# Pairwise outer products with batch norm: how the samples of long rows are cut into stores

## The chip, the cores and the metric

The kernel runs on one core of a Trainium2 chip. The metric is the device time of one execution in microseconds (us); of several executions the median is given.

## The reference, cut to what matters

```python
B, F0, F1, E, C = (256, 39, 39, 16, 1)          # the inputs here have a batch of 1024
_ROWS, _COLS = np.tril_indices(F1, k=-1)        # 741 pairs (row, col) with col < row
cross = xj[:, rows, :, None] * xi[:, cols, None, :]
mean = jnp.mean(cross, axis=(0, 2, 3), keepdims=True)
var = jnp.mean(jnp.square(cross - mean), axis=(0, 2, 3), keepdims=True)
normed = (cross - mean) * jax.lax.rsqrt(var + BN_EPS)
normed = normed * gamma[None, :, None, None] + beta[None, :, None, None]
out = normed[:, :, None, :, :] * W[None, None, :, :, :]
return jnp.transpose(out, (0, 2, 1, 3, 4))
```

xi and xj are 1024 x 39 x 16 in float32. For each of the 741 pairs of fields the outer product of two vectors of 16 is made, normalised with the pair's mean and variance over the batch, and multiplied with a 16 x 16 weight. The output is 1024 x 1 x 741 x 16 x 16, 777 MB, against 6 MB of input. In the output of one sample the pairs of a row r (r pairs: columns 0 to r-1) lie side by side, 1 KB a pair.

## The kernel before, in words

Each of the 128 partitions holds 8 samples. The moments of all pairs are worked out first (until about 40 us), from sums and small matmuls; each pair then has a scale s and a shift t in `st_sb`. What remains is, for each pair and sample, (xi * s) outer xj, plus t, times W, and the store.

**Tiles.** A tile is one row r for two samples of each partition (T = 2): `tiles[n] = (r, t0, place)`. `y_sb` has two slots of 76 pair-places (1 KB a partition each). Tiles 0 to 3 are row 19, tiles 4 to 11 rows 20 and 18; `FIRST_PIECES` sets the cuts of the first eight. From tile 12 on the order is row 38 (four tiles, one for each pair of samples), then rows 37 and 1, 36 and 2, 35 and 3, and so on to 21 and 17, the long row and its short partner together filling a slot. Slots alternate, so a tile's place was used last by the tile before the previous one.

**Steps of a tile.** The program is written in its final order; each engine runs its instructions in that order.

- `scale_xi(n + 2)`: GpSimd multiplies xi with s into an `xs` tile (line 169).
- `finish(n)`: adds t, multiplies by W and stores. For rows over `LONG` (33) ScalarE adds t to 8 pairs in the middle of the row (line 275) and GpSimd multiplies them by W in two steps of four pairs (line 280). For rows 33 and less GpSimd does both for the last 4 pairs or so (lines 277 and 280). All other pairs are VectorE's, one instruction a pair for both samples (line 291), in the order of the pairs.
- `products(n + 1)`: for sample 0, then sample 1, one instruction for each of 16 values of xj; ScalarE does the first 11 or 12 (line 147), GpSimd the rest (line 149). Rows of 4 and less are done by VectorE alone (lines 182 and 192).

**Stores.** SP issues all stores (line 216), in the order of `finish`, on one DMA queue. `bounds(n)` says where a row is cut: two pieces for rows 31 to 38, one for shorter rows. `store(n, c0, c1)` is called at the end of each piece, for the pairs c0 to c1. For a row above 19 from tile 8 on, sample 0 is stored piece by piece and sample 1 in one store behind the last piece:

```python
            if whole and step == 1 and t == t_to - 1:
                if c1 < r:
                    continue
                c0 = 0
```

So a tile of rows 31 to 38 has three stores: first piece of sample 0, second piece of sample 0, all of sample 1. A row below 19 has one store for both samples. In memory one store is one run of bytes for each partition and sample, and the trace has one packet for each such run.

**What sets the order around the change.** Products into a slot wait until the stores of the slot's previous pairs have landed, for each sample's pairs by themselves. A piece's store waits until VectorE and, where its pairs are among them, GpSimd are through with the piece. Products of a sample wait for nothing else of the other sample.

Of the kernel before, what the change touches and what calls it, by code (L numbers as in the profile page):

```python
# [15 lines left out]

ONE, LONG = 30, 33
FIRST_PIECES = (  # L20
    (0, 1, 3, 6, 10, 14, 19), (0, 4, 9, 14, 19), (0, 4, 11, 19), (0, 9, 19), (0, 10, 20), (0, 9, 18), (0, 10, 20), (0, 9, 18)
)
# [18 lines left out]
def tile_pair_outer_batchnorm(  # L41
# [95 lines left out]
    def view(n):  # L137
        r, _, u = tiles[n]
        return y_sb[:, u : u + T * r, :].rearrange("p (t n) e -> p t n e", t=T)
# [65 lines left out]
    def store(n, c0, c1, t_from=0, t_to=T):  # L205
        r, t0, _ = tiles[n]
        n0 = first[r]

        whole = n >= len(FIRST_PIECES)
        step = 1 if r > mid and (whole or c1 == r) else t_to - t_from  # L210
        for t in range(t_from, t_to, step):
            if whole and step == 1 and t == t_to - 1:
# [3 lines that stand above are left out]
            nc.sync.dma_start(  # L216
                out_v[:, t0 + t : t0 + t + step, (n0 + c0) * EE : (n0 + c1) * EE],
                view(n)[:, t : t + step, c0:c1, :].rearrange("p t n e -> p t (n e)"),
            )
# [14 lines left out]
    def weigh(n):  # L234

        y = view(n)
        for c0, c1 in zip(bounds(n), bounds(n)[1:]):
            affine(n, range(c0, min(c1, OWN)), (nc.vector,))
            nc.vector.tensor_tensor(  # L239
                y[:, :, c0:c1, :],  # L240
                y[:, :, c0:c1, :],
                w_dve.unsqueeze(1).to_broadcast([P, T, c1 - c0, EE]),
                ALU.mult,
            )
            store(n, c0, c1)

    def bounds(n):
        if n < len(FIRST_PIECES):
            return FIRST_PIECES[n]
        r = tiles[n][0]  # L250
        pieces = 1 + (r > ONE)
        return tuple(q * r // pieces for q in range(pieces + 1))

    def finish(n):

# [32 lines left out]
        for t in range(0, T, size):  # L288
            for c0, c1 in zip(bounds(n), bounds(n)[1:]):
                for c in [*range(c0, min(c1, p0)), *range(max(c0, p1), c1)]:  # L290
                    stt(  # L291
                        y[:, t : t + size, c, :],
                        y[:, t : t + size, c, :],
                        t_sb[:, n0 + c : n0 + c + 1],
                        w_dve.to_broadcast([P, size, EE]),
                        ALU.add,
                        ALU.mult,
                    )
                store(n, c0, c1, t, t + size)
# [262 lines left out]
```

## Time and profile before

| | |
|---|---|
| median of 4 runs | 1879.26 us (1879.16 to 1880.51) |
| the profiled execution's own time | 1879.28 us |
| its span, first to last instruction or transfer | 1877.6 us |
| VectorE busy | 1723.9 us, 92% |
| ScalarE busy | 1645.8 us, 88% |
| GpSimd busy | 1535.7 us, 82% |
| SP's DMA queue | 779.72 MB in 52320 packets, busy 97.9% of 16 engines' span |
| mean DMA rate over the span | 417 GB/s |

The page is of one execution, taken by the profiler. "Busy" is the time in which an engine executes instructions; DMA shares are those of the core's 16 DMA engines together. A row of the windows view gives a stretch of the span, the busy time of each engine with the number of instructions, the granted TensorE clock, and the share and rate of the DMA engines, where a packet counts in the stretch in which it starts; so a short stretch can show a share a little above 1, or one that is low because long packets began before it. A row of the waits view gives who waited for whom, the total in us, how often, and the longest. The page's table of DMA issues gives the time from a store's issue to its landing, which includes the time it stands in the queue behind others.

### The profile page before, as it was taken

How to read it: one execution, taken by the hardware profiler on the slowest of the kernel's cores; microseconds unless marked ns; L12 is line 12 of the kernel's file. 1: busy time of each engine (PE TensorE's matmuls, PEld its weight loads, DVE VectorE, ACT ScalarE, POOL GpSimd, SP SyncE). 2: the span in 40 equal slices, each digit the busy share in tenths (PEclk: the TensorE clock that was granted, in tenths of full speed). 3: DMA queues.
4: the chain of work that ended last, by engine and by line, in shares of the span. 5: the costliest groups of instructions: out<-in, count | busy, mean ns of one | idle time of the engine just before them, and what ended most of it. 6: DMA issues, size and time to landing. Idle time of an engine off the chain costs nothing.

```text
span 1877.6 us, 9638 instructions
## 1 busy us (share of the span) xinstructions
PE 26.0 (1%) x130; PEld 23.3 (1%) x130; DVE 1723.9 (92%) x2640; ACT 1645.8 (88%) x3416; POOL 1535.7 (82%) x1746
## 2 busy tenths in 40 slices
PE   5000000000000000000000000000000000000000
PEld 4000000000000000000000000000000000000000
DVE  8999888899999999999999999999999999999994
ACT  8999888888888899989999999998999998989892
POOL 8999778787877788888888888888888888888882
DMA  5999999999999999999999999999999999999998
GB/s 200 386 420 424 406 423 425 424 429 426 425 428 426 425 428 426 427 426 425 422 425 432 425 426 431 424 431 424 432 424 431 423 431 428 427 428 426 427 430 349
DMA packets 53690, 783.63 MB, mean 417 GB/s; under 512 B 4720, under 2 KB 6384, under 8 KB 17008
## 3 DMA queue, kind: packets, MB, share of 16 engines
q1 hardware_dynamic: 52320, 779.72, 97.9%
q10 hardware_dynamic: 1296, 3.29, 0.5%
q14 instruction: 73, 0.60, 0.1%
q8 instruction: 1, 0.02, 0.0%
HBM read 6.00 MB, written 776.99 MB: 417 GB/s over the span
## 4 chain that ended last, share of the span: by engine, by line
DMA 55%; ACT 20%; DVE 18%; issue 3%; POOL 2%; SPq 0%; ACTq 0%; DVEq 0%; PE 0%; POOLq 0%
DMA out_dram<-y_sb 55%; ACT y_sb L147 20%; DVE y_sb L291 17%; POOL y_sb L149 1%; DVE y_sb L358 1%; POOL xs L169 0%; ACT y_sb L230 0%; DVE y_sb L332 0%; SPq L216 0%; DMA xi_sb<-in_r_xi_dram 0%; POOL y_sb L277 0%; POOL y_sb L280 0%; POOL y_sb L342 0%; DVE y_sb L192 0%; DVE xs L182 0%
## 5 line engine op out<-in xcount | busy, mean ns | idle before, releaser
L291 DVE SCALAR_TENSOR_TENSOR y_sb<-y_sb,st_sb,w_dve 128x512 f32<-128x512 f32 (+1 forms) x2511 | 1653.2, 739 | 117.4 <-issue 103.8
L147 ACT ACTIVATE y_sb<-xs,xj_sb 128x288 f32<-128x288 f32 (+20 forms) x3194 | 1514.8, 567 | 181.5 <-DMA out_dram<-y_sb 148.4
L149 POOL TENSOR_SCALAR y_sb<-xs,xj_sb 128x480 f32<-128x480 f32 (+27 forms) x1126 | 607.2, 564 | 14.1 <-DMA out_dram<-y_sb 14.0
L280 POOL TENSOR_TENSOR y_sb<-y_sb,w_sb 128x2048 f32<-128x2048 f32 (+3 forms) x155 | 517.8, 3347 | 87.2 <-ACT y_sb L275 77.6
L169 POOL TENSOR_TENSOR xs<-xi_sb,st_sb 128x640 f32<-128x640 f32 (+33 forms) x135 | 184.2, 1364 | 197.1 <-ACT y_sb L147 193.3
L277 POOL TENSOR_SCALAR y_sb<-y_sb,st_sb 128x512 f32<-128x512 f32 x291 | 197.6, 695 | 5.1 <-ACT y_sb L147 5.1
L275 ACT ACTIVATE y_sb<-y_sb,st_sb 128x512 f32<-128x512 f32 x160 | 100.2, 708 | 4.0 <-POOL y_sb L149 2.3
L192 DVE TENSOR_TENSOR y_sb<-xs,ps 128x256 f32<-128x256 f32 (+3 forms) x32 | 24.8, 817 | 0.5
L489 PE MATMUL ps<-y_sb 39*128 39x38 f32 (+37 forms) x76 | 16.4, 397 | 2.8 <-DVE y_sb L475 2.8
L489 PEld LDWEIGHTS ps<-y_sb 39*128 39x128 f32 x76 | 16.3, 329 | 3.1 <-DVE y_sb L475 3.1
L353 ACT ACTIVATE y_sb<-y_sb 128x1248 f32<-128x1248 f32 x8 | 9.9, 1243 | 2.8 <-POOL y_sb L342 1.5
L358 DVE TENSOR_REDUCE y_sb<-y_sb 128x78 f32<-128x1248 f32 x8 | 11.2, 1445 | 0.4 <-ACT y_sb L353 0.4
L147 ACT ACTIVATE y_sb<-xi_sb,xj_sb 128x304 f32<-128x304 f32 x24 | 11.4, 537 | 0.0
L342 POOL TENSOR_TENSOR y_sb<-xi_sb,y_sb 128x1248 f32<-128x1248 f32 x4 | 9.2, 2324 | 2.2 <-ACT y_sb L391 2.2
L239 DVE TENSOR_TENSOR y_sb<-y_sb,w_dve 128x2048 f32<-128x2048 f32 (+4 forms) x6 | 10.7, 1839 | 0.1
L332 DVE TENSOR_REDUCE y_sb<-xi_sb 128x39 f32<-128x624 f32 (+1 forms) x6 | 6.1, 1012 | 3.7 <-DMA xi_sb<-in_r_xi_dram 3.7
L342 POOL TENSOR_TENSOR y_sb<-xj_sb,y_sb 128x1248 f32<-128x1248 f32 x4 | 9.2, 2320 | 0.0
L378 PE MATMUL ps<-y_sb 128*39 128x79 f32 x48 | 8.1, 340 | 15.3 <-DVE y_sb L358 15.1
L232 POOL TENSOR_SCALAR y_sb<-y_sb,st_sb 128x512 f32<-128x512 f32 x8 | 6.5, 817 | 2.1 <-ACT y_sb L147 2.1
L332 DVE TENSOR_REDUCE y_sb<-xj_sb 128x39 f32<-128x624 f32 (+1 forms) x6 | 6.1, 1015 | 0.6 <-DMA xj_sb<-in_r_xj_dram 0.6
L230 ACT ACTIVATE y_sb<-y_sb,st_sb 128x512 f32<-128x512 f32 x9 | 6.5, 802 | 0.2 <-ACT y_sb L147 0.2
L378 PEld LDWEIGHTS ps<-y_sb 128*39 128x39 f32 x48 | 5.8, 178 | 17.3 <-DVE y_sb L358 10.5
(59 smaller groups left out, 37.4 us busy)
## 6 DMA issues: line engine op xcount, KB each, us to landing
out_dram<-y_sb SPq DMA_DIRECT2D x25, 2304.0 KB, 10.4
out_dram<-y_sb SPq DMA_DIRECT2D x12, 3840.0 KB, 21.7
out_dram<-y_sb SPq DMA_DIRECT2D x21, 2048.0 KB, 12.5
out_dram<-y_sb SPq DMA_DIRECT2D x12, 3584.0 KB, 23.1
out_dram<-y_sb SPq DMA_DIRECT2D x12, 3328.0 KB, 24.4
out_dram<-y_sb SPq DMA_DIRECT2D x12, 3072.0 KB, 25.2
out_dram<-y_sb SPq DMA_DIRECT2D x16, 2176.0 KB, 11.0
out_dram<-y_sb SPq DMA_DIRECT2D x8, 4352.0 KB, 24.1
```

The costliest lines, as they stand in the source:

```text
L147: nc.scalar.activation(y, src, AF.Copy, scale=scale)
L149: engine.tensor_scalar(y, src, scale, 1.0, ALU.mult, ALU.mult)
L169: nc.gpsimd.tensor_tensor(xs, xi_sb[:, t0 : t0 + T, 0:r, :], s_sb[:, :, n0 : n0 + r, :].to_broadcast([P, T, r, E]), ALU.mult,)
L192: nc.vector.tensor_tensor(view(n)[:, t].rearrange("p n (i j) -> p n i j", j=E), xs[:, t].unsqueeze(2).to_broadcast([P, r, E, E]), xj_short ...
L275: nc.scalar.activation(y[:, :, c, :], y[:, :, c, :], AF.Identity, bias=t_c)
L277: nc.gpsimd.tensor_scalar(y[:, :, c, :], y[:, :, c, :], t_c, 1.0, ALU.add, ALU.mult)
L280: nc.gpsimd.tensor_tensor(y[:, :, c0:c1, :], y[:, :, c0:c1, :], w_sb.unsqueeze(1).to_broadcast([P, T, c1 - c0, EE]), ALU.mult,)
L291: stt(y[:, t : t + size, c, :], y[:, t : t + size, c, :], t_sb[:, n0 + c : n0 + c + 1], w_dve.to_broadcast([P, size, EE]), ALU.add, ALU.mult,)
L342: nc.gpsimd.tensor_tensor(devs[n % 7], sources[x][:, t0 : t0 + T], shift[:, x : x + 1, :].unsqueeze(3).to_broadcast([P, T, F, E]), ALU.sub ...
L358: nc.vector.tensor_reduce(to[:, t0 : t0 + T, F : 2 * F], devs[n % 7], AX.X, ALU.add)
L378: nc.tensor.matmul(ps_g[acc][0:F, 0 : 2 * F + 1], lhs, fb[:, t], start=t == 0, stop=t == NT - 1)
L489: nc.tensor.matmul(ps[:, :, first[r] - n0 : first[r] - n0 + r], pick[:, r, :], stq[:, :, 0:r], start=True, stop=True,)
```

## The change

Two things in how rows are cut, and nothing in what is computed.

- `store`: the constant `WHOLE` = 36 keeps the scheme "sample 1 in one store" for rows up to 36. In rows 38 and 37 the first piece is now one store for both samples (128 partitions x 2 runs), and the second piece is one store for each sample. These tiles still have three stores.
- `bounds`: in rows 36 to 31 the first piece has 19, 20, 21, 22, 23 and 24 pairs in place of 18, 17, 17, 16, 16 and 15. Rows 38 and 37 are cut as before, at 19 and 18.

```diff
-ONE, LONG = 30, 33
+ONE, LONG, WHOLE = 30, 33, 36
...
-        whole = n >= len(FIRST_PIECES)
+        whole = n >= len(FIRST_PIECES) and r <= WHOLE
         step = 1 if r > mid and (whole or c1 == r) else t_to - t_from
...
         r = tiles[n][0]
-        pieces = 1 + (r > ONE)
-        return tuple(q * r // pieces for q in range(pieces + 1))
+        if r <= ONE:
+            return 0, r
+
+        return 0, r // 2 + max(0, (WHOLE + 1 - r) * 3 // 2), r
```

The order of all instructions on every engine stays as it was, the stores' included; the new file has two more lines inside `bounds`, so the lines behind it are two higher (275 is 277, 280 is 282, 291 is 293), while 147, 149, 169 and 216 stay.

## The prediction

> **What bounds the kernel now.** I read the page first: the span and the DMA rows.
>
> ```profile
> span 1877.6 us, 9638 instructions
> ...
> DMA packets 53690, 783.63 MB, mean 417 GB/s; under 512 B 4720, under 2 KB 6384, under 8 KB 17008
> ## 3 DMA queue, kind: packets, MB, share of 16 engines
> q1 hardware_dynamic: 52320, 779.72, 97.9%
> ```
>
> One queue, SP's, is busy for 97.9% of sixteen engines' span. VectorE with 92% and ScalarE with 88% are high too, but the question is who waits for whom. So the waits come next, ScalarE's first:
>
> ```profile
> ACT y_sb L147 <- DMA out_dram<-y_sb: 148.4, 79, 4.5
> ```
>
> ScalarE's products wait for stores to free their half of y_sb. The loop is closed by the store stream: stores free the buffer, the buffer lets products start, products lead to stores. An edit counts only where it changes the stream's bytes, packets or gaps. For the gaps I cut the steady part into windows (columns: stretch, length, busy time of PE, PEld, DVE, ACT, POOL, clock, DMA share, GB/s):
>
> ```profile
> 191.50:193.30 1.80, 0.00 (x0) 0.00 (x0) 1.03 (x2) 1.80 (x4) 0.35 (x1) 1.00 0.00 0
> 193.30:240.00 46.70, 0.00 (x0) 0.00 (x0) 39.68 (x60) 39.06 (x59) 37.53 (x26) 1.00 1.00 427
> 240.00:240.40 0.40, 0.00 (x0) 0.00 (x0) 0.00 (x0) 0.40 (x1) 0.00 (x0) 1.00 0.00 0
> 240.40:380.00 139.60, 0.00 (x0) 0.00 (x0) 124.01 (x195) 118.94 (x180) 109.58 (x78) 1.00 1.01 427
> 640.00:930.00 290.00, 0.00 (x0) 0.00 (x0) 272.69 (x413) 264.02 (x605) 244.82 (x314) 1.00 1.01 426
> 1500.00:1866.00 366.00, 0.00 (x0) 0.00 (x0) 327.66 (x495) 305.64 (x696) 286.08 (x365) 1.00 1.00 428
> ```
>
> The stream runs at 426 to 428 GB/s everywhere but in two holes, both among the tiles of row 38, where the share is 0.00. Rows 36 to 31 (370 to 930 us) show no hole. The last view is the end, where the share falls although every store is issued:
>
> ```profile
> 1868.00:1870.00 2.00, 0.00 (x0) 0.00 (x0) 0.00 (x0) 0.00 (x0) 0.00 (x0) 1.00 0.27 113
> 1872.00:1874.00 2.00, 0.00 (x0) 0.00 (x0) 0.00 (x0) 0.00 (x0) 0.00 (x0) 1.00 0.10 44
> ```
>
> The trace's sixteen completion marks of each store explain it: twelve engines are done with the last store at 1868.2 to 1868.6, the others up to 1876.7. So the engine that is last sets the end. That engine is late by 0.2 us at 340, by 2 to 3 at 700 to 930 and by 8.4 at the end. A gap hurts only if it reaches that engine.
>
> **Part 1: rows 38 and 37, gain.** The first tile of row 38 starts its finish at 172.69. Its first piece is issued at 184.38 (2432 KB, landing 7.3 us later, at 191.7), its second at 192.56. Landing trails the last packet by 0.4 (the last packet of all ends at 1876.2, its mark is at 1876.7), so the queue is dry from 191.3 until the second piece's first packet at 193.4 (issue 0.33, then 0.5): 2.1 us for all engines. With the change the store at 184.38 carries both samples' first halves, 4864 KB. A half of 2432 KB is 19-KB packets, 8 an engine; at 732 ns each that is 5.9 us, so two last 11.7, from 185.2 to 196.9. The other two issues are where they were (192.56 and 192.94). The hole is gone: -2.1, with -1.8 (the empty window alone) as the lower bound. The hole at 240 is the same thing in the third tile: the piece issued at 231.46 takes 9.2 us, so its last packet ends at 240.2, and the next one starts at 239.64 + 0.33 + 0.5 = 240.5. That is 0.2 for the last engine (0.4 by the window). Together -2.3, between -1.8 and -2.5.
>
> **Part 2: packets, cost.** Row 38 and 37 tiles had three packets a partition (two short, one of the whole sample), and get four short ones: 128 more for each of 8 tiles, 1024, or 64 an engine. The trace's packet records give 1448.4 ns for 38912 B and 731.6 for 19456 B (means), so a cut costs 2 x 731.6 - 1448.4 = 14.8 ns. 64 x 14.8 = +0.95 us. From the fastest packets it is 2 x 721 - 1436 = 6 ns, +0.4; I take the means, since most packets run in a full stream. The number of DMA instructions stays three a tile, and SP's queue holds them in the same order.
>
> The Trainium skill has a rule against such cuts: its page "DMA: Bandwidth & Descriptors" (section Bandwidth, Measured) puts a floor of about 10.5 ns on a packet. By it the 64 packets would be 0.67 us, an estimate from that page, and the forecast 0.3 us lower. The page's figure is for small loads, the row is for these stores, so the row stands.
>
> **Part 3: sample 0 comes free later, cover.** ScalarE and GpSimd make products of sample 0 first. Before, sample 0 of a tile left the queue in its first half of bytes; now it leaves after three quarters, 5.9 us later relative to the tile's end. Sample 1's time does not move. Before, ScalarE found sample 0 free and waited 2.5 to 4.4 us before sample 1 (rows at 211.96, 234.94 and 258.46); that wait moves ahead of sample 0 and becomes longer. On ScalarE's queue the sample-1 products stand behind it and then the next tile's eight L275 steps; VectorE and GpSimd wait for those. Worked out for row 38, from the landing of sample 0: 2 x 7.73 (eleven products each) + 0.1 + 11.7 (finish start to first store, 172.69 to 184.38; GpSimd's two L280 steps end last) + 0.83 (issue to first packet) = 28.1. The stream has from that landing the last piece (5.9) and the whole next tile (four such halves, 23.4), less the 0.4 by which landing trails: 28.9. Spare 0.8; with row 37's products of 7.57 it is 1.1. Before, the tightest place was the second piece, with nothing spare at 240. So the cover is thin but whole: 0, and if it is gone the loss is the overrun, once in two tiles.
>
> **Part 4: rows 36 to 31, later first pieces, cover.** First pieces grow from 18, 17, 17, 16, 16, 15 pairs to 19, 20, 21, 22, 23, 24. For rows 36 to 34 VectorE's share becomes 11, 12 or 13 pairs (x 0.66 = 7.3 to 8.6 us), still earlier than GpSimd's 11.7, so the issue does not move. For rows 33, 32 and 31 VectorE alone decides, and the issue moves by 6, 7 and 9 pairs: 4.0, 4.6 and 5.9 us. The cover is the queue ahead of them. A store into an idle queue lands 7.2 us after issue where its packets take 5.9, so 1.3 is overhead. The first pieces of row 33 land 11.7 to 13.5 us after issue; less 1.3 and their own 4.95 the last engine reaches them after 5.4 or more: 1.4 spare. Row 32: 12.7 to 14.5, 6.4 or more, 1.8 spare. Row 31: 14.2 to 14.8 with 4.65 of its own, 8.2 or more, 2.3 spare. The early engines will run dry there for up to a microsecond or two; they are not the last. Packets in number are unchanged. The second piece is issued as before, and follows more bytes: no gap. Cost 0; if the last engine ran dry too, up to 1 us a tile.
>
> **Sum.** The profiled execution took 1879.28, span 1877.6 and 1.7 around it; the median of the runs is 1879.26, the same. 1879.3 - 2.3 + 0.95 = 1877.95; with the bounds (-2.5 + 0.4, -1.8 + 0.95) 1877.2 to 1878.4. I say 1878.0, 0.07% less: the holes are all that a store's shape can fill here.
>
> **Rivals.** First, slower: part 3's chain is longer than its rows. The first store of a row 38 or 37 tile then comes after the queue is dry, for the last engine too. It decides from 0.8 us of overrun; beyond that each microsecond is lost once in two tiles, about three times from the third tile to the last of row 37. An overrun of 3 gives 3 x 2.2 - 1.3 = +5.3, 1884.6. For it: the spare is small, and the two-sample pieces with 256 packets in these tiles are new. Against: two-sample stores of 18-KB packets ran in 150 to 184 us at full rate, and every term has a row.
>
> Second, nothing gained: the hole is filled but opens one tile later, as the tiles behind are not ready; only the packets stay, 1880.2. Against: the second tile's first piece is issued at 205.90, and the first tile's bytes now last until about 209.
>
> Third, much faster: the last engine's 8.4 us are evened out in part. Half of it would give 1878.0 - 4.2 = 1873.8. Against: the stores load all engines alike before and after, so nothing evens them.
>
> **How the numbers follow.** A measurement of this kernel tells about 0.2% (3.8 us) from no change. Forecast 0.70 and second rival 0.10, both within it: 0.80. First rival 0.14, slower. Third 0.06, faster. The range takes in the forecast's bounds, the second rival and small overruns: 1876.4 to 1881.5, leaving out most of the first and third.
>
> **What would show it.** Right: no window with share 0.00 between 185 and 242, the second tile of row 38 starting to stream at about 209, ScalarE's waits standing before sample 0 in rows 38 and 37, first stores of rows 33 to 31 landing about 10 to 12 us after issue, larger as they are, in place of 12 to 15. Wrong: windows below full rate between 230 and 380 (first rival), a hole after 209 (second), a tail shorter than 8 us (third), or holes at 650 to 930 that the end feels.

## The result and the profile after

The changed kernel takes 1877.27 us (median of 41 runs, 1876.81 to 1878.64), the kernel before 1879.46 (61 runs). The ratio is 0.9988, 95% interval 0.9984 to 0.9993: 2.2 us less, between 1.3 and 3.0. The forecast was 1.3 less.

The page after, the rows that answer to those of before:

```profile
span 1875.9 us, 9638 instructions
...
DMA packets 54714, 783.63 MB, mean 418 GB/s; under 512 B 4720, under 2 KB 6384, under 8 KB 17520
## 3 DMA queue, kind: packets, MB, share of 16 engines
q1 hardware_dynamic: 53344, 779.72, 98.1%
```

There are 1024 packets more (53690 became 54714), as counted. The waits, and the windows of before on the trace after:

```profile
ACT y_sb L147 <- DMA out_dram<-y_sb: 142.2, 77, 4.4
```

```profile
191.50:193.30 1.80, 0.00 (x0) 0.00 (x0) 1.53 (x3) 1.80 (x3) 0.85 (x2) 1.00 1.21 519
193.30:240.00 46.70, 0.00 (x0) 0.00 (x0) 39.69 (x60) 39.12 (x59) 37.51 (x26) 1.00 1.00 426
240.00:240.40 0.40, 0.00 (x0) 0.00 (x0) 0.00 (x0) 0.40 (x2) 0.00 (x0) 1.00 0.81 340
240.40:380.00 139.60, 0.00 (x0) 0.00 (x0) 124.15 (x195) 119.49 (x180) 110.82 (x78) 1.00 1.00 425
640.00:930.00 290.00, 0.00 (x0) 0.00 (x0) 272.74 (x414) 264.11 (x601) 244.73 (x316) 1.00 1.01 426
...
1868.00:1870.00 2.00, 0.00 (x0) 0.00 (x0) 0.00 (x0) 0.00 (x0) 0.00 (x0) 1.00 0.20 87
...
1872.00:1874.00 2.00, 0.00 (x0) 0.00 (x0) 0.00 (x0) 0.00 (x0) 0.00 (x0) 1.00 0.08 35
```

Both windows that had a share of 0.00 are filled (1.21 and 0.81). The rates elsewhere are those of before, and the tail is there as before, 1.6 us earlier. ScalarE's timeline shows the move of its wait (start, length, engine, line, operation, in brackets the idle time before and who ended it). The first two rows are of before, the others of the changed kernel:

```profile
199.88 7.73 ACT L147 ACTIVATE y_sb<-xs,xj_sb 128x608 f32<-128x608 f32 x11 [0.66 <-DMA out_dram<-y_sb]
211.96 7.72 ACT L147 ACTIVATE y_sb<-xs,xj_sb 128x608 f32<-128x608 f32 x11 [4.36 <-DMA out_dram<-y_sb]
...
203.96 15.34 ACT L147 ACTIVATE y_sb<-xs,xj_sb 128x608 f32<-128x608 f32 x22 [4.26 <-DMA out_dram<-y_sb]
219.39 5.01 ACT L277 ACTIVATE y_sb<-y_sb,st_sb 128x512 f32<-128x512 f32 x8
227.63 15.35 ACT L147 ACTIVATE y_sb<-xs,xj_sb 128x608 f32<-128x608 f32 x22 [3.23 <-DMA out_dram<-y_sb]
```

Both samples' products now run as one block of 22 instructions behind the wait. Before, the wait stood between two blocks of 11.

To place the gain I took the sixteen completion marks of each store in the traces, and measured (in us) from the last store ahead of row 38 to the last store of rows 38 and 37 (first of the two stretches), and from there to the end. "Median" is the median of the sixteen marks, "last" the latest one.

| kernel | rows 38, 37: median | last | the rest: median | last |
|---|---|---|---|---|
| before | 190.3 | 190.2 | 1493.2 | 1500.5 |
| changed | 187.9 | 188.0 | 1493.1 | 1500.6 |
| rows 38 and 37 alone | 187.8 | 187.8 | 1493.4 | 1500.9 |
| first pieces alone | 190.3 | 190.2 | 1493.0 | 1500.4 |
| first tile alone | 189.4 | 189.3 | 1493.2 | 1500.4 |
| row 38 alone | 189.5 | 189.4 | 1493.3 | 1500.4 |
| all rows in halves | 187.9 | 187.8 | 1497.6 | 1503.7 |

The gain is in rows 38 and 37, 2.3 to 2.4 us; the rest is unchanged within 0.2. (The span shows 1.7 because the start before row 38 was 0.5 us longer in the execution that was profiled.)

### The profile page after: what moved, and what is told of

Read it like the earlier page. It is cut to its first block, busy times and chain, and to the rows that moved or that the text cites. A ratio compares the mean times of both kernels' runs of the same rounds, so it can differ in the third digit from the quotient of the medians.

```text
span 1875.9 us, 9638 instructions
## 1 busy us (share of the span) xinstructions
PE 26.0 (1%) x130; PEld 23.3 (1%) x130; DVE 1723.9 (92%) x2640; ACT 1645.7 (88%) x3416; POOL 1535.6 (82%) x1746
## 2 busy tenths in 40 slices
DMA packets 54714, 783.63 MB, mean 418 GB/s; under 512 B 4720, under 2 KB 6384, under 8 KB 17520
## 4 chain that ended last, share of the span: by engine, by line
DMA 38%; ACT 13%; DVE 7%; issue 1%; POOL 0%; SPq 0%; ACTq 0%; DVEq 0%; POOLq 0%
DMA out_dram<-y_sb 38%; ACT y_sb L147 13%; DVE y_sb L293 7%; POOL xs L169 0%; SPq L216 0%; ACTq L147 0%; DVEq L559 0%; DVE st_sb L509 0%; DVE ps L502 0%; DVE st_sb L508 0%; DVEq L293 0%; POOLq L169 0%
## 5 line engine op out<-in xcount | busy, mean ns | idle before, releaser
L147 ACT ACTIVATE y_sb<-xs,xj_sb 128x288 f32<-128x288 f32 (+20 forms) x3194 | 1514.1, 568 | 179.5 <-DMA out_dram<-y_sb 142.2
```

The costliest lines, as they stand in the source:

```text
L147: nc.scalar.activation(y, src, AF.Copy, scale=scale)
```

## The experiments

**Rows 38 and 37 alone.** From the changed kernel:

```diff
-        return 0, r // 2 + max(0, (WHOLE + 1 - r) * 3 // 2), r
+        return 0, r // 2, r
```

> Rows 38 and 37 stored in halves of both samples, rows 36 to 31 cut as before. Theory (the stream of the last DMA engine, with its holes at 191 and 240 us, sets the end): this half of the change is all of it, 1.8 to 2.4 us under before, and no stretch with DMA share 0.00 between 185 and 242. Rival (the longer first pieces bring part of it, by a steadier stream at 650 to 930): 1.2 us under before or less, and the rest in the run with the first pieces alone.

Measured: 1877.39 (before on the same chip 1879.30), ratio 0.9989, interval 0.998 to 0.9998: 1.9 us under before. The windows at the two holes:

```profile
191.50:193.30 1.80, 0.00 (x0) 0.00 (x0) 0.77 (x2) 1.80 (x4) 0.05 (x1) 1.00 1.22 519
240.00:240.40 0.40, 0.00 (x0) 0.00 (x0) 0.00 (x0) 0.40 (x2) 0.00 (x0) 1.00 1.14 486
```

This half of the change is all of it within 0.3 us, as the theory said.

**First pieces alone.**

```diff
-        whole = n >= len(FIRST_PIECES) and r <= WHOLE
+        whole = n >= len(FIRST_PIECES)
```

> First pieces of rows 36 to 31 grown to 19 to 24 pairs, rows 38 and 37 stored as before. Theory: no change, within 0.5 us of before; both holes (191.5 to 193.3 and 240.0 to 240.4) stand as before; first stores of rows 33 to 31 reach the queue 4 to 6 us later, without effect on the end. Rival: 1 us under before or better.

Measured: 1879.36 against 1879.30, ratio 0.9999, interval 0.999 to 1.0008. Both holes stand:

```profile
191.50:193.30 1.80, 0.00 (x0) 0.00 (x0) 1.21 (x2) 1.80 (x4) 0.51 (x1) 1.00 0.00 0
240.00:240.40 0.40, 0.00 (x0) 0.00 (x0) 0.00 (x0) 0.40 (x2) 0.00 (x0) 1.00 0.01 0
```

Longer first pieces are worth nothing here; the queue in front of them covers the later issue.

**First tile alone.** Cuts of rows 36 to 31 as before, and

```diff
-        whole = n >= len(FIRST_PIECES) and r <= WHOLE
+        whole = n >= len(FIRST_PIECES) and n != 12
```

> Only the first tile of row 38 is stored in halves of both samples; all others as before. Theory: the hole at 191 is filled (-2.1 us), packets cost 0.1, but the third tile of row 38 is bound by its sample 0, which now comes free after three quarters of the first tile; its second piece is issued at about 239 and the queue is dry from about 237.5: a hole of 1.3 us opens at 238 to 239, and the net is 0.6 to 0.9 us under before. Rival (a hole that is filled stays filled, the other tiles follow the stream): 2.0 us under before.

Measured: 1878.46 against 1879.30, 0.8 us under before; the ratio 0.9995 (0.9987 to 1.0004) does not exclude no change, so the verdict rests on the trace. Two windows of it:

```profile
191.50:193.30 1.80, 0.00 (x0) 0.00 (x0) 1.27 (x2) 1.80 (x3) 0.58 (x1) 1.00 0.86 368
...
238.00:239.00 1.00, 0.00 (x0) 0.00 (x0) 0.98 (x2) 1.00 (x2) 0.27 (x1) 1.00 0.01 0
```

The hole at 191 is filled and another opens at 238 to 239, where it was expected. Filling one hole puts the stream two microseconds ahead, and the third tile of row 38, which is stored in the old way, is then late for it: its second piece is issued at 239.00, only 0.6 us earlier than before, and its first store brings only a quarter of a tile.

**Row 38 alone.** As before that, with

```diff
-        whole = n >= len(FIRST_PIECES) and r <= WHOLE
+        whole = n >= len(FIRST_PIECES) and r < 38
```

> Only row 38 (four tiles) is stored in halves of both samples, row 37 and the cuts of rows 36 to 31 as before: 512 fewer packets than the rows-only run (-0.5 us). Theory (the hole moves to the first tile that is stored in the old way while its products waited for a tile stored in the new way): a hole of 0.6 to 0.9 us at 284 to 285, in the first tile of row 37, and about the same time as the rows-only run, 1.5 to 1.9 us under before. Rival (the hole at 191 was all): 2.4 us under before.

Measured: 1878.69 against 1879.36, ratio 0.9996 (0.9987 to 1.0005): 0.7 under before, less than either expected. The hole has moved to the first tile of row 37:

```profile
284.20:285.20 1.00, 0.00 (x0) 0.00 (x0) 0.97 (x4) 1.00 (x2) 1.00 (x2) 1.00 0.05 18
```

It is where it was expected, but costs more than reckoned (1.2 us of idle time for an engine, by the packet records), and another of 0.8 follows in row 37's second tile at 309, where the kernel before has 0.3. The table agrees: the stretch of rows 38 and 37 is 0.8 under before, where the whole change has 2.3.

**All rows in halves.** Cuts of rows 36 to 31 as before, `WHOLE` = 30:

```diff
-ONE, LONG, WHOLE = 30, 33, 36
+ONE, LONG, WHOLE = 30, 33, 30
```

> All rows 38 to 31 stored in halves of both samples, cuts of rows 36 to 31 as before: against the rows-only run 128 more packets in each of 24 tiles, 3072, or 192 an engine, and the same number of stores. Theory with the prediction's price (14.8 ns for a packet): 2.8 us over the rows-only run, 0.9 over before. Price from the fastest packets (6 ns): 1.2 us over the rows-only run. Rival (a cut costs nothing in a full queue; the prediction's term was the wrong one): within 0.4 us of the rows-only run. No new hole is expected in any of them.

Measured: 1880.29 against 1879.22 of before on its chip: 1.1 over before (ratio 1.0006, 0.9997 to 1.0015), which puts it about 3 us over the rows-only run, as the theory said. The rate of 640 to 930 is a little lower, without a hole. But behind the last of the 24 tiles, where row 30 begins, which is stored in the old way, there is a hole that was not expected. The first two rows are of this run, the third of the rows-only run:

```profile
640.00:930.00 290.00, 0.00 (x0) 0.00 (x0) 271.59 (x411) 260.51 (x601) 243.26 (x308) 1.00 1.01 425
935.50:938.00 2.50, 0.00 (x0) 0.00 (x0) 2.50 (x5) 2.50 (x6) 2.50 (x4) 1.00 0.16 69
935.50:938.00 2.50, 0.00 (x0) 0.00 (x0) 2.08 (x4) 2.50 (x6) 0.04 (x1) 1.00 0.97 417
```

So the 3 us are not the packets alone. From the end of row 37 to the last store of row 31, that is, ahead of this hole, the median mark falls 1.7 us and the last mark 2.0 us behind the rows-only run. For 192 packets an engine that is 9 to 10 ns for a packet, or 11 by the median if one adds a hole of 0.4 us at 401 that only the rows-only run has. The rest, 2.6 us at the median mark and 1.0 at the last, comes in the first tile of row 30. The total agreed with the price of 14.8 by luck.

**The cover taken away.** The changed kernel with rows 33 to 31 in one piece:

```diff
-ONE, LONG, WHOLE = 30, 33, 36
+ONE, LONG, WHOLE = 33, 33, 36
```

> The changed kernel, but rows 33 to 31 have one piece (sample 0 whole, then sample 1 whole), so that their first store is issued only when the whole row is done: 7.9 to 8.6 us later than before the change, where the last engine reached it after 5.4 to 8.2. Theory (cover of the last engine, then one loss in two tiles): 5.4 us of holes for the last engine in the first tiles of rows 33 and 32, 1.4 less by 96 fewer packets an engine: 4 us over the changed kernel, 1.8 over before. Rival A (the early engines' dry time sets the end): 8 us over the changed kernel or more. Rival B (the queue covers that too): 1 us under the changed kernel.

Measured: 1884.61 against 1879.30, ratio 1.0028 (1.0017 to 1.0039): 5.3 over before, 7.3 over the changed kernel. The stretch of these rows:

```profile
640.00:930.00 290.00, 0.00 (x0) 0.00 (x0) 265.64 (x403) 257.72 (x589) 237.47 (x304) 1.00 0.97 415
655.00:657.00 2.00, 0.00 (x0) 0.00 (x0) 2.00 (x4) 2.00 (x4) 1.73 (x3) 1.00 0.00 0
703.00:705.60 2.60, 0.00 (x0) 0.00 (x0) 2.60 (x5) 2.60 (x6) 2.37 (x4) 1.00 0.41 167
```

290 us at 415 in place of 426 GB/s lose 7.5 us, which is the whole difference. So the cover is real: once first stores come 8 us later, the queue is dry. But it was nearer Rival A's number than the theory's. I had reckoned holes in the first tiles of rows 33 and 32 alone; by the packet records most engines stand idle ahead of the first store in eight of the twelve tiles (3.9 us in the first, 0.3 to 1.7 in the others). The rule "lost once in two tiles" was wrong here.

**Why a few DMA engines end late.** Two runs send the very last store as two DMAs over part of the partitions each (108 and 20; 120 and 8):

```diff
-            nc.sync.dma_start(
+            for p0, p1 in ((0, 108), (108, P)) if n == len(tiles) - 1 else ((0, P),):
+                nc.sync.dma_start(
...
```

> The changed kernel, but the very last store (row 17, 2 x 17 KB a partition) is made of two DMAs, of partitions 0 to 107 and 108 to 127. By the Trainium skill's page DMA: Bandwidth & Descriptors (section on why a DMA increments its semaphore by 16) a DMA is spread over the largest number up to 16 that divides its partitions, on the lowest-numbered engines: 12 and 10 here, which leaves four engines without a share. Theory (the end is set by the few engines that are late, whatever the others do): where the late engines are among those left out, they end 10.4 us earlier (16 packets of 0.65) and the loaded ones 3.9 later (6 packets), so the end is 4 to 5 us earlier. Where they are among the loaded ones, the end is 3.9 us later. Rival (the tail is the landing of the last store as a whole, not of late engines): no change beyond 0.5 us.

> The changed kernel, but the very last store is made of two DMAs, of partitions 0 to 119 and 120 to 127; by the same rule as in the run with 108 partitions 15 engines and 8, which leaves one engine without a share of it and gives eight engines two packets more. Theory: if the engine left out is the last one, the end moves to the next-late one, 1.5 to 2.8 us earlier; if the last one is among the eight, 1.3 later; otherwise no change. Rival (no late engines): no change beyond 0.5 us.

Measured: 1883.59 (ratio 1.0023, 1.0014 to 1.0032) and 1887.16 (1.0041, 1.0028 to 1.0055), 6.3 and 9.9 us over the changed kernel; neither theory had that. The tail of the run with 120:

```profile
1866.00:1868.00 2.00, 0.00 (x0) 0.00 (x0) 0.00 (x0) 0.00 (x0) 0.00 (x0) 1.00 0.98 263
1868.00:1870.00 2.00, 0.00 (x0) 0.00 (x0) 0.00 (x0) 0.00 (x0) 0.00 (x0) 1.00 0.68 174
```

In the first of these windows the engines are 98% busy and move 263 GB/s. With 120, 127 of the last 256 packets of 17 KB take over 1 us in the records (up to 2.8), with 108 30 of them (up to 1.6); in the changed kernel none takes over 0.66. The two DMAs have 13 and 11 completion marks in the run with 108, 16 and 9 in the run with 120: one more than the engines that the rule in the expectations gives (12 and 10, 15 and 8). So the engines were left out as planned, but with a store over part of the partitions packets became slower. Why is not shown, and these runs do not tell who is late. The third run leaves the stores alone and gives the idle TensorE more instructions:

```diff
+            if n > 12:
+                for _ in range(30):
+                    nc.tensor.matmul(banks[0][0:E, 0:E], xi_sb[:, 0, 0, :], xi_sb[:, 0, 1, :], start=True, stop=True)
```

> The changed kernel with 30 small matmuls (16 x 16, of xi with itself, into a bank of PSUM that nothing reads) behind each tile from the fourteenth on: 4170 matmuls on an engine that is otherwise idle from 60 us on. They touch no store and no wait. Theory: the late DMA engines are late by instruction loads. In the trace before, four engines end 8.4, 5.9, 4.5 and 2.5 us after the other twelve; ScalarE has 3416 instructions, VectorE 2640, GpSimd 1746, which is 27, 21 and 14 loads of 8 KB at 64 bytes each, and a load's record is 309 ns: 8.3, 6.4 and 4.2 us. TensorE's 8340 more are 65 loads, 20 us on one engine: if that is one of the twelve, the end moves by 20 - 8.7 = 11 to 12 us, if it is one of the four by 14 to 20. Rival (lateness has nothing to do with instruction loads): no change beyond 0.5 us.

Measured: 1911.07, ratio 1.0169 (1.0155 to 1.0183), 33.8 us over the changed kernel. Three rows of its page, and the stretch in which the matmuls ran, in this run and after the change:

```profile
span 1909.5 us, 26318 instructions
...
DVE  8998778888999999999999999999999999999994
...
q8 instruction: 66, 1.08, 0.2%
```

```profile
50.00:470.00 420.00, 228.82 (x8331) 223.75 (x8327) 355.60 (x569) 350.10 (x606) 331.02 (x290) 0.68 0.95 393
50.00:470.00 420.00, 0.00 (x0) 0.00 (x0) 386.84 (x617) 375.80 (x646) 358.02 (x313) 1.00 1.00 421
```

VectorE, ScalarE and GpSimd are busy as long as before (1724.0, 1646.0 and 1532.3 us), but VectorE's digits up to about 480 us are thinner than after the change: there the matmuls ran ahead, and their instructions were loaded. 66 loads made 1.08 MB, 16 KB each, not 8 as I had taken. The instructions added were 16680 (26318 against 9638), not 8340, so the number of loads came out at 65 all the same. At the stores' rate for one engine (17408 B in 648 ns) the added 1.06 MB are 39 us of one engine's time.

The marks show how this reached the end. While the loads run, to 468 us, the last mark of a store is 4.0 to 10.5 us behind the median one (0.1 to 1.3 after the change). The other engines do not get further ahead, since products wait for the last mark of a store (ScalarE waits 178.7 us for stores in all, against 142.2). At the end of row 36, at 497 us, the median mark is already 30.3 us later than after the change, and at the end of the program 33.4. So the whole stream waited for what was held up, and it lost most of those 39 us. The four late engines at the end are as far behind the others as they were (8.7 us for the last), so the 8.7 that the theory took off plays no part. The matmuls ran at the same time as their loads and were not run without them; that mainly one mark of the sixteen lags fits loads, which are one packet each. That the four late engines of the kernel itself are late because of instruction loads fits their instruction counts, but no run took loads away, and which engine serves whose loads the trace does not record.

## Why the prediction was right, point by point

**What bounds.** Right. The stream of stores bounds the kernel, and only its bytes, packets and holes count: a half of the change that fills holes is all of the gain, one that only moves issues under the queue's cover is worth nothing, and one that opens holes (rows 33 to 31 in one piece) costs what the rate shows. That the stream had only two holes was not right: one of 0.3 us at 310, in row 37, and one of 0.7 at 936, where row 30 begins (just behind the stretch that was called free of holes), were there too. The second stays after the change. Both are in the trace before:

```profile
309.00:310.20 1.20, 0.00 (x0) 0.00 (x0) 1.17 (x4) 1.20 (x3) 1.20 (x2) 1.00 0.69 292
935.00:936.50 1.50, 0.00 (x0) 0.00 (x0) 1.50 (x3) 1.50 (x3) 1.50 (x3) 1.00 0.59 244
```

**Part 1, the holes: right in kind, short in size.** This is the term that was mis-sized: 2.3 us in the sum, about 3.1 in the traces. Both holes are gone, and the stretch of rows 38 and 37 is 2.3 to 2.4 us shorter although it has more packets. I had measured each hole at the engine that was last there: 2.1 and 0.2. At the median mark the holes are longer. At 191 it landed at 191.5, so, with the landing's 0.4, the queue was dry from 191.1 to 193.4: 2.3. At 240 it is 0.7, as the median had landed at 240.2 and the last at 240.6. A third of 0.35, from 309.9 in row 37, the last engine of that moment did not have at all. Together 3.4. The packet records, counted by how many run at each moment, give nearly the same: between 186 and 380 us an engine (the mean of sixteen) has no packet for 3.3 us before and for 0.2 after. The step that failed is "A gap hurts only if it reaches that engine". The lag of the last engine is not kept in this stretch: it comes and goes, 0.1 to 1.0 us before and 0.1 to 1.3 after, and it is 0.9 and 1.0 at the end of row 37. What the last engine saved at a hole was lost again, and what the twelve see is the better measure here. Which engine a mark belongs to is not recorded.

**Part 2, packets: too dear.** The prediction had 14.8 ns for a packet, or 0.95 us. The run with all rows in halves gives 9 to 11 ns where it has no hole. Rows 38 and 37 give 10 to 12: 3.1 us less idle and 2.3 to 2.4 us gained leave 0.7 to 0.8 for 64 packets. The mean lengths of packet records, from which 14.8 came, do not give the price so finely: the medians of the same records give 12 (2 x 728 - 1444), the fastest 6. The 10.5 ns that the prediction takes from the Trainium skill's page agrees with these runs, though it is for small loads, and the argument that the row stands against it was wrong.

**Part 3, sample 0.** Right, and as thin as said. In the trace after, the first stores of the third tile of row 38 and the later ones find the queue with 0 to 1.1 us left, and no hole. The first rival, slower, did not come: no term of the chain was longer than its row. What it said of losses, once in two tiles, was not tested in these rows; in the run with one piece it was wrong.

**Part 4, first pieces.** Right: no effect on the end, and first stores of rows 33 to 31 land 9.6 to 11.8 us after issue in place of 11.7 to 14.8 (a piece of row 31 issued at 863 lands after 10.9, the one issued at 859 before after 14.2). The engines stand idle for 0.1 us each in these rows (by the packet records, 640 to 930), where the prediction allowed the early ones a microsecond or two.

**The other rivals.** "Filled here, open a tile later" was put at 0.10 as no gain; it did not happen to the change, but it is just what happened with the first tile or row 38 alone, and at row 30 with all rows in halves. The change escapes because row 37 goes along; in row 36 only 0.2 us open, at 402 (0.4 in the rows-only run, at 401). The third, a shorter tail, did not come: the last engine is 8.7 us behind after the change, 8.4 before.

The forecast of 1.3 less was 0.9 short of the measured 2.2, and at the edge of the measurement's interval. By the traces about 0.8 of this comes from Part 1 and 0.2 from Part 2.

## What to carry to other kernels

Where a transfer queue is full, look for the windows in which it is empty, and price a change by these windows and by its packets; the rest of its effect is cover. A larger first store fills a hole, but puts the stream ahead of the work behind it, so the same cut has to go on until that work has room, or the hole moves. Measure a hole at the median engine and at the last one; here the truth lay nearer the first, while the engines ran in step. And look behind the last tile that is cut in the new way: a hole there is easily taken for the price of the packets.

## What the runs showed of the hardware

A store cut into one more packet costs about 10 ns in a full queue (10 to 12 for 19 KB, 9 to 11 for 15 to 18 KB). Loads of instructions run beside the stores: with 16680 more instructions on an engine that is otherwise idle (65 more loads, 1.06 MB) the last mark was 4.0 to 10.5 us behind the median while they ran, and the kernel took 33.8 us more. Where the last store was split over 108 and 20, or 120 and 8 partitions, packets of 17 KB took up to 1.6 and 2.8 us in place of 0.65.
